# A graph network's first projection: seven half products for a pair of tiles, and counts shared between two engines

## The chip, the cores and the metric

The kernel runs on one core of one Trainium2 chip. The engines named here are TensorE (PE in the profile; PEld are its weight loads), VectorE (DVE), ScalarE (ACT), GpSimd (POOL) and SyncE (SP), which only issues DMAs. Each engine works through its own queue in order. The metric is device time in microseconds (us) of one execution; 10 runs of the kernel before the change had a median of 5349.94 us (5346.88 to 5354.68).

## The reference, cut to what matters

Two graph attention layers over 10,000 nodes with 170,000 edges (self loops among them, and one more a node in each layer), fp32, each with a residual product and layer norms. The change touches the first projection only, and the preparation of the edge lists that runs beside it:

```python
xl = (x @ W).reshape(n, heads, out_ch)          # x: 10000 x 768, W1: 768 x 1024
alpha_src = jnp.einsum('nhc,hc->nh', xl, a_src)  # 4 heads of 256
alpha_dst = jnp.einsum('nhc,hc->nh', xl, a_dst)
e = jax.nn.leaky_relu(alpha_src[src] + alpha_dst[dst], 0.2)
```

## The kernel before, in words

The nodes lie in NT = 79 tiles of 128 rows. The first stage (lines 602 to 670) makes `table1`: for each node the 1024 products with W1 plus b1, and 4 + 4 sums with a_dst and a_src. Then two stages gather rows of the tables by edge lists and do the rest; the change does not touch them.

The first stage is written out by hand: within `manual_schedule()` each engine's instructions stand in the order of the code. For each tile t:

- TensorE: `product` (L171) multiplies x's six transposed blocks of 128 x 128 with W1 (`w1`, held in SBUF) in two halves of 512 columns, 12 fp32 matmuls. PSUM has room for two such results (`ps_big`), so TensorE can be one tile ahead.
- ScalarE copies the result into `row` (L657). VectorE multiplies it in PSUM with a_dst and a_src spread over the partitions (L660, into `scr`, two buffers), and ScalarE sums each head's 256 numbers (L663, four per product, each with a readout of the accumulator).
- GpSimd adds b1 to `row` (L665). SyncE stores the row (L667). SyncE's load of x for tile t + 2 (`load_x`, L610, three buffers) stands ahead of that store.
- `next(steps)` (L668) then gives out one step of the preparation (`prepare`, L190) and one of the weights (`weight_steps`, L627). These steps stand in the same queues, between one tile's work and the next's. They come in this order: step 3 reads the edges' targets on VectorE and loads W2 on SyncE, step 4 makes a table of 1408 block ends by eleven transposes (L216, L217); steps 5 to 31 make 80 counts of how many block ends lie below a node's number, three in a step (L239, one pass over 1408 numbers on VectorE, summed by the instruction), turn them into addresses (`at`, L241), have GpSimd gather the blocks (L244) and look at the blocks of the step before (`remainder`, L230, L232). Steps 4 to 19 also multiply a block of W2 on VectorE (L642) and sum it on ScalarE (L643); step 19 loads Wr1, step 20 multiplies br1 with W2 on TensorE (L646). Steps 32 to 40 sort nodes by degree (L276, and L323 to L330 in groups with products on TensorE), steps 37 to 50 scatter the order with GpSimd's DMAs, six in a step (L313); steps 52 to 56 read it back on SyncE in pieces of 16 bytes (L344) and store ranks (L347); steps 57 to 76 gather the lists of sources, four DMAs of GpSimd in a step (L392), and VectorE works on them (`listed`, L365) a step later.

Of the kernel before, what the change touches and what calls it, by code (L numbers as in the profile page):

```python
# [79 lines left out]
def gnn_kernel(ctx, tc, x, x_cols, src, dst, src_col, dst_col, W1, a_src1, a_dst1, b1, g1, be1, Wr1, br1,  # L80
# [109 lines left out]
    def prepare():  # L190

        with tc.tile_pool(name="prep", bufs=1, side="right") as pool, \
                tc.tile_pool(name="prep2", bufs=2, side="right") as pool2:
            rows = pool.tile([P, NA, P], I32, name="rows")
            nc.sync.dma_start(rows, bass.AP(tensor=dst.tensor, offset=0, ap=[[P, P], [P * P, NA], [1, P]]))
            nxt = pool.tile([P, NA, P], I32, name="nxt")
            nc.sync.dma_start(nxt, bass.AP(tensor=dst.tensor, offset=1, ap=[[P, P], [P * P, NA], [1, P]]))
            info = pool.tile([P, NT, 4], I32, name="info")
            nc.vector.memset(info, 0)
# [1 line left out]
                nc.sync.dma_start(d.rearrange("(p j) f -> p (j f)", p=P), info.rearrange("p j f -> p (j f)"))  # L201
            yield
            yield
            fall = pool2.tile([P, NA * P], F32, name="less", bufs=1).rearrange("p (a e) -> p a e", e=P)
            nc.vector.tensor_tensor(fall, rows, nxt, op=OP.subtract)
            wrong = pool.tile([P, 3], F32, name="wrong")
            nc.vector.reduce_max(wrong[:, 0:1], fall.rearrange("p a e -> p (a e)"), axis=AX.X)
# [6 lines left out]
            for a in range(NA):  # L214
# [4 lines left out]
            ids = pool.tile([P, NB], F32, name="ids")  # L219
            nc.gpsimd.iota(ids, pattern=[[1, NB]], base=0, channel_multiplier=NT,  # L220
                           allow_small_or_imprecise_dtypes=True)
            whole = pool.tile([P, NB], F32, name="whole")
            rest = pool.tile([P, NB], F32, name="rest")
            at = pool.tile([P, NB], I32, name="at")
# [10 lines left out]
            for j in range(0, NB, STEP):  # L235
                m = min(STEP, NB - j)
                for i in range(j, j + m):
                    less = pool2.tile([P, NA * P], F32, name="less", bufs=1)
                    nc.vector.tensor_scalar(less, most.rearrange("p a e -> p (a e)"), ids[:, i:i + 1], 0.0,  # L239
                                            op0=OP.is_lt, op1=OP.add, accum_out=whole[:, i:i + 1])  # L240
                nc.vector.tensor_copy(at[:, j:j + m], whole[:, j:j + m])  # L241
                chunk = pool2.tile([P, STEP, P], I32, name="chunk")
                for i in range(m):
                    nc.gpsimd.indirect_dma_start(  # L244
                        out=chunk[:, i, :], out_offset=None, in_=dst.rearrange("(c e) o -> c (e o)", e=P),
                        in_offset=bass.IndirectOffsetOnAxis(ap=at[:, j + i:j + i + 1], axis=0))
                for r in asked:
                    remainder(*r)
                asked = [(j, m, chunk)]
                yield  # L250
            for r in asked:
# [18 lines left out]
            hot = pool.tile([P, NT, D], BF16, name="hot")  # L270
            nc.vector.tensor_tensor(hot, key[:, :, None].to_broadcast([P, NT, D]),
                                    node[:, None, :D].to_broadcast([P, NT, D]), op=OP.is_equal)
            before = pool.tile([P, NT + 1, D], BF16, name="before")
            nc.vector.memset(before[:, 0, :], 0.0)
            for j in range(NT):
                nc.vector.tensor_add(before[:, j + 1, :], before[:, j, :], hot[:, j, :])  # L276
# [9 lines left out]
            facts = pool.tile([P, NT, 4], I32, name="facts")  # L286
# [9 lines left out]
            base = each  # L296
            s = 1
            while s < D:
                more = pool.tile([P, D], F32, name=f"more{s}")
# [38 lines left out]
            yield  # L338

            sorted_ = pool.tile([P, NT, 4], I32, name="sorted_")  # L340
            others = [pool.tile([P, NT, 4], I32, name=n) for n in ("rows", "nxt", "info")]
# [258 lines left out]
    w2, wr1 = (wp.tile([P, k, n], F32, name=s) for s, k, n in (("w2", K1, R2), ("wr1", K0, C1)))  # L600

    with tc.tile_pool(name="w1", bufs=1) as w1p, tc.tile_pool(name="l1", bufs=2) as io, \
            psum_for_products(), tc.manual_schedule():
        w1 = w1p.tile([P, K0, C1], F32, name="w1")
        xTs = {}

        def load_x(t):
            if t < NT:
                xTs[t] = io.tile([P, K0, P], F32, name="xT", bufs=3)
                nc.sync.dma_start(xTs[t], x_cols[t])  # L610
# [16 lines left out]
        def weight_steps():  # L627

            with nc.allow_non_contiguous_dma(reason="1024 numbers"):
                nc.scalar.dma_start(br1_c, br1.rearrange("(k p) -> p k", p=P))
            yield
            yield
            brT = spread_br1(w1p, "brT")
            load(w2, W2)
            for i, a in enumerate((a_dst2, a_src2)):
                vec = spread(w1p, a, "a2")
                for k in range(K1):
                    yield  # L640
                    m = io.tile([P, C1], F32, name="scr")[:, :C2]
                    nc.vector.tensor_mul(m, w2[:, k, :C2], vec)  # L642
# [3 lines left out]
            q = product(brT, w2, R2)  # L646
            row = io.tile([P, R1], F32, name="row")
            nc.scalar.copy(row[:, :R2], q[:, :R2])
            nc.vector.tensor_add(lift, row[:, C2:C2 + 1], row[:, C2 + 1:R2])
            nc.scalar.dma_start(shift, row[0:1, :C2])  # L650


        steps = itertools.zip_longest(prepare(), weight_steps())
        for t in range(NT):
            p = product(xTs.pop(t), w1, C1)
            row = io.tile([P, R1], F32, name="row")
            nc.scalar.copy(row[:, :C1], p[:, :C1])  # L657
            for i, vec in enumerate((ad_b, as_b)):
                m = io.tile([P, C1], F32, name="scr")
                nc.vector.tensor_mul(m, p[:, :C1], vec)  # L660
# [4 lines left out]
            nc.gpsimd.tensor_add(row[:, :C1], row[:, :C1], b1_b)  # L665
            load_x(t + 2)
            nc.sync.dma_start(table1[t * P:(t + 1) * P, :R1 - 1], row[:, :R1 - 1])  # L667
            next(steps, None)  # L668
        for _ in steps:
            pass  # L670
# [613 lines left out]
```

## Time and profile before

| what | us |
| --- | --- |
| median of 10 runs | 5349.94 |
| the profiled execution, whole | 5356.32 |
| its span, first to last instruction | 5354.5 |
| last ScalarE sum of the first stage ends | 885.7 |
| TensorE busy with the tiles' products (L171, W1), 1896 records | 826.7 |
| VectorE's counts (L239), 80 of 1676 ns | 134.1 |
| GpSimd's bias adds (L665), 79 of 2369 ns | 187.2 |
| ScalarE's head sums (L663), 632 of 402 ns, and their readouts, 632 of 187 ns | 253.5 and 117.9 |

A tile's product with W1 has two records for each fp32 matmul, so 24. A row of the timeline reads: start, duration, engine and line, operation, output<-input, shapes, and in brackets how long the engine was idle just before and which event ended that. A name with a q (SPq) is an engine's queue issuing a DMA. The table by stretch gives for each stretch of the span the busy time of each engine, the granted clock of TensorE and what the DMA engines did. The view of DMA issues gives the size and the median time from issue to landing.

### The profile page before, as it was taken

What the parts mean: (1) busy time and instruction counts of PE and PEld (TensorE: products, weight loads), DVE (VectorE), ACT (ScalarE), POOL (GpSimd) and SP (SyncE); (2) the same over time, 40 slices, a digit from 0 to 9 for tenths busy, and PEclk for the clock granted to TensorE, in tenths of its full rate; (3) what the DMA queues carried; (4) which work ended last, traced back from release to release, by engine and by line L of the source; (5) the groups of instructions that cost most, each with busy time, mean ns of one, the idle gap of its engine ahead of it and who ended that gap; (6) DMA issues with size and microseconds to landing.
All of it is one profiled execution on the core that took longest, in us unless ns stands there. A gap on an engine that the chain in (4) does not pass through costs nothing. (4 is left out here: it accounts for less than half of the span.)

```text
span 5354.5 us, 59565 instructions
## 1 busy us (share of the span) xinstructions
PE 4762.7 (89%) x15188; PEld 2853.2 (53%) x15191; DVE 4283.1 (80%) x7729; ACT 2799.0 (52%) x8184; POOL 3227.1 (60%) x3159
## 2 busy tenths in 40 slices
PE   8999997999999886578999999999998865889998
PEld 3444443555555544345555555566665544566665
DVE  4884244899999888688899999689988767889998
ACT  3434343677778776577878777433333222323332
POOL 3446455455666654556666655277777656777774
PEclk9999998999999988789999999999999887999999
DMA  4333625899999997699999999599999989999995
GB/s 156 124 101 84 97 87 190 313 335 345 360 362 361 360 333 293 237 326 342 351 366 364 356 338 335 179 386 376 376 370 346 328 269 321 330 353 371 365 387 218
DMA packets 474306, 1591.37 MB, mean 297 GB/s; under 512 B 118327, under 2 KB 122487, under 8 KB 473958
## 3 DMA queue, kind: packets, MB, share of 16 engines
q0 software_dynamic: 322384, 1286.62, 66.3%
q1 hardware_dynamic: 149520, 297.43, 16.7%
q10 hardware_dynamic: 2054, 3.42, 0.2%
q8 instruction: 128, 2.10, 0.2%
q14 instruction: 220, 1.80, 0.1%
HBM read 1431.80 MB, written 177.29 MB: 301 GB/s over the span
## 5 line engine op out<-in xcount | busy, mean ns | idle before, releaser
L424 POOL DMA_INDIRECT ring<-table,slots x2675 | 2647.3, 990 | 1438.9 <-DVE acc L519 337.7
L519 DVE SCALAR_TENSOR_TENSOR acc<-ring,e,acc 128x512 f32<-128x512 f32 (+1 forms) x2530 | 1578.0, 624 | 126.2 <-PE acc L729 50.7
L508 ACT ACTIVATE ring<-ring,e 128x256 f32<-128x256 f32 x3284 | 1337.4, 508 | 0.0
L515 DVE TENSOR_TENSOR acc<-acc,ring 128x1024 f32<-128x1024 f32 x801 | 985.6, 1230 | 79.5 <-ACT ring L508 10.6
L928 PE MATMUL big<-ring,diagonals 128*128 128x256 f32 x2754 | 679.1, 409 | 203.4 <-ACT diagonals L927 194.3
L171 PE MATMUL big<-w,xT 128*128 128x512 f32 x1896 | 826.7, 598 | 27.2 <-DMA w<-in_W_dram 9.8
L171 PE MATMUL big<-wr,xT 128*128 128x512 f32 x1896 | 832.5, 596 | 0.2 <-ACT xT L700 0.2
L817 PE MATMUL half<-w,hT 128*128 128x512 f32 (+1 forms) x2528 | 830.4, 486 | 0.0
L942 PE MATMUL big<-wr,w 128*128 128x512 f32 (+1 forms) x2464 | 823.2, 487 | 0.0
L928 PEld LDWEIGHTS big<-ring,diagonals 128*128 128x128 f32 x2754 | 559.1, 206 | 320.5 <-ACT diagonals L927 222.2
L817 PEld LDWEIGHTS half<-w,hT 128*128 128x128 f32 x2528 | 477.8, 189 | 372.7 <-issue 310.0
L729 PE MATMUL acc<-ring,diagonals 128*128 128x256 f32 x1912 | 484.3, 412 | 212.0 <-ACT diagonals L723 212.0
L942 PEld LDWEIGHTS big<-wr,w 128*128 128x128 f32 x2464 | 469.7, 191 | 329.9 <-issue 298.0
L171 PEld LDWEIGHTS big<-w,xT 128*128 128x128 f32 x1896 | 362.3, 192 | 487.6 <-issue 468.3
L171 PEld LDWEIGHTS big<-wr,xT 128*128 128x128 f32 x1896 | 356.2, 191 | 419.9 <-issue 419.3
L729 PEld LDWEIGHTS acc<-ring,diagonals 128*128 128x128 f32 x1912 | 391.8, 208 | 296.9 <-ACT diagonals L723 234.5
L576 ACT ACTIVATE sd<-mv,eps 128x1 f32<-128x1 f32 x237 | 69.6, 294 | 821.6 <-DVE mv L574 821.5
L927 ACT ACTIVATE diagonals<-ident,e 128x128 f32<-128x128 f32 x1377 | 411.1, 387 | 142.1 <-DVE e L499 129.7
L660 DVE TENSOR_TENSOR scr<-big,ad_b 128x1024 f32<-128x1024 f32 x79 | 96.7, 1224 | 380.7 <-ACT row L657 380.7
L723 ACT ACTIVATE diagonals<-ident,e 128x128 f32<-128x128 f32 x956 | 292.8, 387 | 203.6 <-DVE e L499 203.2
L485 ACT ACTIVATE e<-e 128x68 f32<-128x68 f32 (+29 forms) x160 | 38.2, 239 | 659.8 <-DVE e L484 631.8
L665 POOL TENSOR_TENSOR row<-row,none 128x1024 f32<-128x1024 f32 x79 | 187.2, 2369 | 267.3 <-ACT row L657 266.9
(172 smaller groups left out, 3614.0 us busy)
## 6 DMA issues: line engine op xcount, KB each, us to landing
ring<-table,slots POOLq DMA_INDIRECT x2675, 6.9
table<-row SPq DMA_DIRECT2D x79, 516.0 KB, 3.7
h_d<-hT SPq DMA_DIRECT2D x79, 512.0 KB, 6.8
w<-h_d SPq DMA_DIRECT2D x77, 512.0 KB, 8.5
table<-row SPq DMA_DIRECT2D x79, 385.0 KB, 7.2
ring<-table SPq DMA_DIRECT2D x79, 385.0 KB, 6.6
xT<-in_x_cols_dram SPq DMA_DIRECT2D x79, 384.0 KB, 4.5
x_d<-xt SPq DMA_DIRECT2D x79, 384.0 KB, 7.6
```

The costliest lines, as they stand in the source:

```text
L171: nc.tensor.matmul(p[:, c:e], aT[:, j, :], w[:, j, c:e], start=(j == 0), stop=(j == k - 1))
L424: nc.gpsimd.indirect_dma_start(out=to, out_offset=None, in_=table, in_offset=bass.IndirectOffsetOnAxis(ap=index, axis=0), **more)
L508: nc.scalar.activation(row[:, s], row[:, s], AF.Copy, scale=e[:, h:h + 1])
L515: nc.vector.tensor_add(acc[:, :c], acc[:, :c], row[:, :c])
L519: nc.vector.scalar_tensor_tensor(acc[:, s], row[:, s], e[:, h:h + 1], (acc if first is None else first)[:, s], op0=OP.mult, op1=OP.add)
L665: nc.gpsimd.tensor_add(row[:, :C1], row[:, :C1], b1_b)
L723: nc.scalar.activation(diagonals[:, k * H1 + i, :], ident, AF.Copy, scale=e[:, k, i:i + 1])
L729: nc.tensor.matmul(acc[:, c:d], diagonals[:, k * H1 + i, :], ring.slot(q + k)[:, c:d], start=(k == 0 and c % BANK == 0), stop=(k == m - 1 ...
L817: nc.tensor.matmul(q, hT[:, j, :], w2[:, j, c:c + q.shape[1]], start=(j == 0), stop=(j == K1 - 1))
L927: nc.scalar.activation(diagonals[:, k % G, :], ident, AF.Copy, scale=e[:, k, :])
L928: nc.tensor.matmul(to, diagonals[:, k % G, :], ring.slot(FIRST[t] + k)[:, ON_PE2:C2], start=False, stop=(k == n - 1), skip_group_check=True)
L942: nc.tensor.matmul(r[:, c:d], hT[:, j, :], wr2[:, j, c:d], start=False, stop=(j == K1 - 1 and (d < C2 or not whole(t))), skip_group_check= ...
```

## The change

The rows of two tiles (t, t + 1), the two halves of the 768 inputs and the two halves of the 1024 columns make a 2 x 2 by 2 x 2 product of blocks. Strassen's scheme makes it from seven half products (3 matmuls of 512 columns each, 21 for two tiles in place of 24), each of a sum or difference of blocks of x with one of blocks of W1. Tile 0 is done alone, then 39 pairs.

- W1's five sums and differences are made once on VectorE, two of them in place after tile 0's product.
- x's five sums and differences (128 x 384 each) are made on VectorE for each pair, one pair ahead (`pair`).
- The seven results are combined on VectorE with seven additions or subtractions of 128 x 512 and on ScalarE with two copies. The seventh product is added by TensorE to m1's bank after m1 was read. Six PSUM banks (`ps_m`) take the place of the two double ones; `row` has four buffers.
- `finish` does what followed the product before, now from `row` in SBUF. The loads of x for the next pair stand behind the first two products of this pair.
- In each count step the counts with an even number are made on ScalarE: `Sign` with the sum of the instruction, then a short `Copy` that turns the sum of signs into a count. The output that nobody reads (`less`) is bf16 with two buffers.
- br1's product with W2 uses the new banks, and `brT` a buffer of `scr`. Some tiles of the preparation share buffers by taking each other's names.

```diff
             for j in range(0, NB, STEP):
                 m = min(STEP, NB - j)
                 for i in range(j, j + m):
-                    less = pool2.tile([P, NA * P], F32, name="less", bufs=1)
-                    nc.vector.tensor_scalar(less, most.rearrange("p a e -> p (a e)"), ids[:, i:i + 1], 0.0,
-                                            op0=OP.is_lt, op1=OP.add, accum_out=whole[:, i:i + 1])
+                    less = pool2.tile([P, NA * P], BF16, name="less")
+                    if i % 2:
+                        nc.vector.tensor_scalar(less, most.rearrange("p a e -> p (a e)"), ids[:, i:i + 1], 0.0,
+                                                op0=OP.is_lt, op1=OP.add, accum_out=whole[:, i:i + 1])
+                        continue
+                    nc.scalar.activation(less, most.rearrange("p a e -> p (a e)"), AF.Sign, scale=-1.0,
+                                         bias=halves[:, i:i + 1], accum_out=whole[:, i:i + 1])
+                    nc.scalar.activation(whole[:, i:i + 1], whole[:, i:i + 1], AF.Copy, bias=0.5 * NA * P, scale=0.5)
                 nc.vector.tensor_copy(at[:, j:j + m], whole[:, j:j + m])
...
-        for t in range(NT):
-            p = product(xTs.pop(t), w1, C1)
-            row = io.tile([P, R1], F32, name="row")
-            nc.scalar.copy(row[:, :C1], p[:, :C1])
...
+        def finish(t, row):
             for i, vec in enumerate((ad_b, as_b)):
                 m = io.tile([P, C1], F32, name="scr")
-                nc.vector.tensor_mul(m, p[:, :C1], vec)
+                nc.vector.tensor_mul(m, row[:, :C1], vec)
                 for h in range(H1):
                     s = slice(h * DH1, (h + 1) * DH1)
                     nc.scalar.activation(m[:, s], m[:, s], AF.Copy,
                                          accum_out=row[:, C1 + i * H1 + h:C1 + i * H1 + h + 1])
             nc.gpsimd.tensor_add(row[:, :C1], row[:, :C1], b1_b)
+            nc.sync.dma_start(table1[t * P:(t + 1) * P, :R1 - 1], row[:, :R1 - 1])
...
+        def times(a, b, p=None):
+            to = ps_m.tile([P, BANK], F32, name="m")[:, :NH] if p is None else p
+            for k in range(a.shape[1]):
+                nc.tensor.matmul(to, a[:, k, :], b[:, k, :], start=(p is None and k == 0),
+                                 stop=(k == a.shape[1] - 1), skip_group_check=True)
+            return to
...
+        bsums = w1p.tile([P, 3, KH, NH], F32, name="bsums")
+        for to, a, op, b in ((bsums[:, 0], b11, OP.add, b22), (bsums[:, 1], b11, OP.add, b12),
+                             (bsums[:, 2], b21, OP.add, b22), (b12, b12, OP.subtract, b22),
+                             (b21, b21, OP.subtract, b11)):
+            nc.vector.tensor_tensor(to, a, b, op=op)
+        finish(0, row)
+        next(steps, None)
+
+        def pair(t):
+            a1, a2 = (xTs.pop(i) for i in (t, t + 1))
+            a11, a12, a21, a22 = (a[:, k, :] for a in (a1, a2) for k in (upper, lower))
+            sums = io.tile([P, 5, KH, P], F32, name="sums")
+            for i, (a, op, b) in enumerate(((a11, OP.add, a12), (a21, OP.add, a22), (a11, OP.add, a22),
+                                            (a21, OP.subtract, a11), (a12, OP.subtract, a22))):
+                nc.vector.tensor_tensor(sums[:, i], a, b, op=op)
+            return a11, a22, sums
+
+        ready = pair(1)
+        for t in range(1, NT, 2):
+            a11, a22, sums = ready
+            r1, r2 = new_row(), new_row()
+            m3 = times(a11, b12)
             load_x(t + 2)
-            nc.sync.dma_start(table1[t * P:(t + 1) * P, :R1 - 1], row[:, :R1 - 1])
+            m5 = times(sums[:, 0], b22)
+            nc.scalar.copy(r1[:, right], m5)
+            load_x(t + 3)
+            m2 = times(sums[:, 1], b11)
+            nc.scalar.copy(r2[:, left], m2)
+            nc.vector.tensor_sub(r2[:, right], m3, r2[:, left])
+            m4 = times(a22, b21)
+            nc.vector.tensor_sub(r1[:, left], m4, r1[:, right])
+            nc.vector.tensor_add(r1[:, right], r1[:, right], m3)
+            nc.vector.tensor_add(r2[:, left], r2[:, left], m4)
+            if t + 2 < NT:
+                ready = pair(t + 2)
+            m1 = times(sums[:, 2], bsums[:, 0])
+            nc.vector.tensor_add(r2[:, right], r2[:, right], m1)
+            m6 = times(sums[:, 3], bsums[:, 1])
+            nc.vector.tensor_add(r2[:, right], r2[:, right], m6)
+            times(sums[:, 4], bsums[:, 2], m1)
+            nc.vector.tensor_add(r1[:, left], r1[:, left], m1)
+            finish(t, r1)
+            next(steps, None)
+            finish(t + 1, r2)
             next(steps, None)
```

More of the change, by code (lines that the diff above doesn't have):

```diff
@@ L193, in prepare @@
                 tc.tile_pool(name="prep2", bufs=2, side="right") as pool2:
-            rows = pool.tile([P, NA, P], I32, name="rows")
+            both = pool.tile([P, 2, NA, P], I32, name="hot")
+            rows, nxt = both[:, 0], both[:, 1]
             nc.sync.dma_start(rows, bass.AP(tensor=dst.tensor, offset=0, ap=[[P, P], [P * P, NA], [1, P]]))
-            nxt = pool.tile([P, NA, P], I32, name="nxt")
             nc.sync.dma_start(nxt, bass.AP(tensor=dst.tensor, offset=1, ap=[[P, P], [P * P, NA], [1, P]]))
@@ L203, in prepare @@
             yield
-            fall = pool2.tile([P, NA * P], F32, name="less", bufs=1).rearrange("p (a e) -> p a e", e=P)
+            fall = pool.tile([P, NA, P], F32, name="most")
             nc.vector.tensor_tensor(fall, rows, nxt, op=OP.subtract)
@@ L221, in prepare @@
                            allow_small_or_imprecise_dtypes=True)
+            halves = pool.tile([P, NB], F32, name="halves")
+            nc.vector.tensor_scalar_add(halves, ids, -0.5)
             whole = pool.tile([P, NB], F32, name="whole")
@@ L272, in prepare @@
                                     node[:, None, :D].to_broadcast([P, NT, D]), op=OP.is_equal)
-            before = pool.tile([P, NT + 1, D], BF16, name="before")
+            before = pool.tile([P, NT + 1, D], BF16, name="most")
             nc.vector.memset(before[:, 0, :], 0.0)
@@ L285, in prepare @@
             nc.vector.tensor_scalar(lower, node, number, None, op0=OP.is_gt)
-            facts = pool.tile([P, NT, 4], I32, name="facts")
+            facts = pool.tile([P, NT, 4], I32, name="info")
             nc.vector.memset(facts, 0)
@@ L298, in prepare @@
             while s < D:
-                more = pool.tile([P, D], F32, name=f"more{s}")
+                more = pool.tile([P, D], F32, name="more", bufs=2)
                 nc.vector.tensor_add(more[:, :D - s], base[:, :D - s], base[:, s:])
@@ L340, in prepare @@
             sorted_ = pool.tile([P, NT, 4], I32, name="sorted_")
-            others = [pool.tile([P, NT, 4], I32, name=n) for n in ("rows", "nxt", "info")]
+            others = [pool.tile([P, NT, 4], I32, name=n) for n in ("hot", "most", "info")]
             with nc.allow_non_contiguous_dma(reason="16 bytes a node"):
@@ L602, in gnn_kernel @@
     with tc.tile_pool(name="w1", bufs=1) as w1p, tc.tile_pool(name="l1", bufs=2) as io, \
-            psum_for_products(), tc.manual_schedule():
+            tc.tile_pool(name="ps_m", bufs=6, space=PSUM) as ps_m, \
+            tc.tile_pool(name="ps_tr", bufs=2, space=PSUM) as ps_tr, tc.manual_schedule():
         w1 = w1p.tile([P, K0, C1], F32, name="w1")
@@ L634, in weight_steps @@
             yield
-            brT = spread_br1(w1p, "brT")
             load(w2, W2)
@@ L645, in weight_steps @@
             yield
-            q = product(brT, w2, R2)
-            row = io.tile([P, R1], F32, name="row")
-            nc.scalar.copy(row[:, :R2], q[:, :R2])
+            brT = spread_br1(io, "scr")
+            row = io.tile([P, R1], F32, name="row", bufs=4)
+            for c in range(0, R2, BANK):
+                q = ps_m.tile([P, BANK], F32, name="m")[:, :min(BANK, R2 - c)]
+                for k in range(K1):
+                    nc.tensor.matmul(q, brT[:, k, :], w2[:, k, c:c + q.shape[1]],
+                                     start=(k == 0), stop=(k == K1 - 1))
+                nc.scalar.copy(row[:, c:c + q.shape[1]], q)
             nc.vector.tensor_add(lift, row[:, C2:C2 + 1], row[:, C2 + 1:R2])
@@ L653, in gnn_kernel @@
         steps = itertools.zip_longest(prepare(), weight_steps())
-        for t in range(NT):
-            p = product(xTs.pop(t), w1, C1)
-            row = io.tile([P, R1], F32, name="row")
-            nc.scalar.copy(row[:, :C1], p[:, :C1])
+        KH, NH = K0 // 2, C1 // 2
+        assert NT % 2 and K0 % 2 == 0 and NH <= BANK
+        upper, lower = slice(0, KH), slice(KH, K0)
+        left, right = slice(0, NH), slice(NH, C1)
+        b11, b12, b21, b22 = (w1[:, k, n] for k in (upper, lower) for n in (left, right))
+        def finish(t, row):
             for i, vec in enumerate((ad_b, as_b)):
                 m = io.tile([P, C1], F32, name="scr")
-                nc.vector.tensor_mul(m, p[:, :C1], vec)
+                nc.vector.tensor_mul(m, row[:, :C1], vec)
                 for h in range(H1):
@@ L665, in gnn_kernel, with new_row @@
             nc.gpsimd.tensor_add(row[:, :C1], row[:, :C1], b1_b)
-            load_x(t + 2)
-            nc.sync.dma_start(table1[t * P:(t + 1) * P, :R1 - 1], row[:, :R1 - 1])
+            nc.sync.dma_start(table1[t * P:(t + 1) * P, :R1 - 1], row[:, :R1 - 1])
+        def new_row():
+            return io.tile([P, R1], F32, name="row", bufs=4)
+        def times(a, b, p=None):
[4 more added lines that the diff above has]
+            return to
@@ new lines, in gnn_kernel @@
+        row = new_row()
+        x0 = xTs.pop(0)
+        for n in (left, right):
+            nc.scalar.copy(row[:, n], times(x0, w1[:, :, n]))
+        load_x(2)
+        bsums = w1p.tile([P, 3, KH, NH], F32, name="bsums")
[3 more added lines that the diff above has]
+            nc.vector.tensor_tensor(to, a, b, op=op)
```

## The prediction

> **What bounds the kernel now.** The change lies in the first stage: the last of the tiles' ScalarE sums ends at 885.7 us of the span of 5354.5. I read the table by stretch first, for the engine that is never idle there.
>
> ```profile
> core 0: us, PE busy (x) PEld busy (x) DVE busy (x) ACT busy (x) POOL busy (x), PEclk, DMA share, GB/s
> 150.00:200.00 50.00, 47.03 (x109) 20.06 (x108) 39.91 (x54) 22.37 (x79) 24.94 (x19) 1.00 0.33 108
> 550.00:600.00 50.00, 50.00 (x118) 22.07 (x117) 11.78 (x10) 21.57 (x85) 25.21 (x19) 1.00 0.33 86
> ```
>
> TensorE is busy throughout in the quiet stretch, at clock 1.00. Early, VectorE is at 80%: there the counts run. The timeline shows who ends a tile there (VectorE, one tile):
>
> ```profile
> 131.35 1.22 DVE L660 TENSOR_TENSOR scr<-big,ad_b 128x1024 f32<-128x1024 f32 x1 [1.90 <-ACT row L657]
> 132.49 1.21 DVE L660 TENSOR_TENSOR scr<-big,as_b 128x1024 f32<-128x1024 f32 x1
> 133.62 1.67 DVE L239 TENSOR_SCALAR_CACHE_REDUCE less<-most,ids 128x1408 f32<-128x1408 f32 x1
> ...
> 138.78 0.17 DVE L241 CAST at<-whole 128x3 int32<-128x3 f32 x1
> 138.89 0.56 DVE L230 TENSOR_TENSOR below<-chunk,ids 128x384 f32<-128x384 int32 x1
> 139.48 0.55 DVE L232 TENSOR_REDUCE rest<-below 128x3 f32<-128x384 f32 x1
> 139.95 0.95 DVE L642 TENSOR_TENSOR scr<-w,a 128x768 f32<-128x768 f32 x1
> 142.80 1.22 DVE L660 TENSOR_TENSOR scr<-big,ad_b 128x1024 f32<-128x1024 f32 x1 [1.90 <-ACT row L657]
> ```
>
> One tile takes 11.45 us (131.35 to 142.80) while counts and the sums over W2 both run. Elsewhere it is the 10.30 us of SyncE's stores, which also show SyncE's order: store, then the load for a later tile.
>
> ```profile
> 576.35 0.33 SPq L667 DMA_DIRECT2D table<-row  x1
> 576.77 0.38 SPq L610 DMA_DIRECT2D xT<-in_x_cols_dram  x1
> 586.65 0.33 SPq L667 DMA_DIRECT2D table<-row  x1
> 587.07 0.38 SPq L610 DMA_DIRECT2D xT<-in_x_cols_dram  x1
> ```
>
> **What TensorE saves.** 1896 records are 79 tiles x 12 products x 2 passes: 10.30/24 = 0.429 us a pass. A pair goes from 48 passes (20.6) to 42 (18.02): 2.58 x 39 = 101 us, if TensorE stays the bound.
>
> **Why it doesn't: a closed loop in each pair.** By the diff's order, the seventh product adds into m1's bank, so it waits for VectorE's add of m1. That add is queued behind the five sums of the next pair. They need x of the next two tiles, whose loads are issued in this same pass of the loop, on SyncE behind the store of the previous pair's second row. That store waits for GpSimd's bias add, which now waits for VectorE's two products (they read the row, no longer PSUM), which wait for the last add of the previous pair's seventh product. Before, the load was issued two tiles ahead and nothing on TensorE waited for VectorE except to reuse PSUM. So a pair lasts as long as the longer of TensorE (18.02), the VectorE chain V and the load chain X, with 0 = start of a pair's first 128x1024 product.
>
> Prices. A 128x1024 product: next starts 1.14 later; 128x512 from PSUM: 0.68 (row of L326), 0.60 with the overlap of 0.08; 128x384: 0.55, so 0.47. Four ScalarE sums: 121.16 to 122.77 = 1.61. Bias add 2.37. A count on ScalarE is not in the trace: from L663 and L643 (0.40 a piece at 256, 0.84 at 768: 0.86 ns an element) 1408 gives 1.39, and with the accumulator's 0.1 and the short Copy's 0.2 I take 1.7; bounds 1.2 and 2.1 from the 1.0 of a 1024 copy (L657) and twice L643. A count on VectorE 1.72, the rest of a count step 0.11 + 1.06. That `less` is now bf16 I cost at nothing: at half of L239's time VectorE would only wait longer for ScalarE's counts; the shared buffer names move no instruction. VectorE to TensorE 0.2 (L217 to L216).
>
> Common end: add of m1 0.65 + 0.2 + seventh product 2.58 + its add 0.60 = 4.0. V = (VectorE or ScalarE free after the second step) + four combinations 2.4 + five sums 2.35 + 4.0 = that + 8.8.
> X: the second store starts at B; store and load issue 0.42 each; landing of the second load; four sums 1.9; 4.0. The view of DMA issues:
>
> ```profile
> xT<-in_x_cols_dram SPq DMA_DIRECT2D x79, 384.0 KB, 4.5
> wr<-in_Wr_dram SPq DMA_DIRECT2D x2, 3072.0 KB, 10.2
> w<-in_W_dram SPq DMA_DIRECT2D x1, 3072.0 KB, 13.5
> ```
>
> Each 4.5 stands behind one store; the second of two loads also has the first ahead of it, 384 KB, so I take 5.2 (bounds: the 3.7 of the quickest xT, the 8.5 of ad_b). X = B + 0.84 + 5.2 + 5.9 = B + 12.0.
>
> **Pairs, by what preparation puts between the rows.**
> - Counts alone (pairs 11-14): products to 2.28; ScalarE's sums to 4.47. Step 1: two VectorE counts to 5.7, one ScalarE count to 6.15, rest to 7.3. Products to 9.6; ScalarE's sums to 11.8, its two counts to 15.2, where VectorE waits 3.9; rest to 16.4. V = **25.2** (20.6 before). The moved counts bring VectorE nothing: it waits for them, behind ScalarE's sums.
> - Counts and W2 sums (3-8): 0.87 twice on VectorE, 0.84 on ScalarE, behind which m5's and m2's copies (0.5 + 0.6) stand: those end at 20.2. V = **29.0** (22.9).
> - Scatters (19-24): GpSimd's order in the timeline is
>
> ```profile
> 445.65 2.36 POOL L665 TENSOR_TENSOR row<-row,none 128x1024 f32<-128x1024 f32 x1 [1.26 <-ACT row L657]
> 448.17 0.99 POOL L313 DMA_INDIRECT order_d<-facts,to  x1 [0.16 <-issue]
> ...
> 456.81 2.36 POOL L665 TENSOR_TENSOR row<-row,none 128x1024 f32<-128x1024 f32 x1 [1.29 <-ACT row L657]
> ```
>
>   First add 2.4 to 4.8, six scatters of 1.27 to 12.5, second add: B = 14.9, X = **26.9**.
> - Source lists (29-38): four gathers of 1.26 in place of the six: B = 12.35, X = **24.3**; V = 13.4 + 5.8 = 19.2 is shorter.
> - Quiet (25): `scr` has two buffers, so the third product waits for ScalarE to 3.0, the fourth to 4.6; second add 5.8 to 8.2; with one scatter B = 8.5, X = **20.5**, hardly under 20.6.
> - Single ones. Pair 1: W2's load (13.5) stands before x: 30. Pair 2: eleven transposes wait for VectorE, then a count: 27.5. Pair 9: Wr1's load (10.2): 31.6. Pair 10: the product with W2 (10.4) starts only after the first count step, at 8.0, then m3 to m7: 37.2. Pair 15: two counts in step 2: 23.5. Pair 16: 17.2 + 9.2 of small VectorE steps (375.54 to 392.74; 395.00 to 404.18), V = 4.6 + 26.4 + 8.8 = 39.8. Pair 17: 6.5 of them, B = 13.5: 25.5. Pair 18: 7.1, B = 14.5: 26.5. Pairs 26, 27: 16-byte loads before each store and load, which held SyncE 6 us each (597.86, 6.71): 30 each. Pair 28: the store of ranks, whose followers landed 21.2 later: 34.4.
>
> **The sum.** Pair 1's first product starts near 48: tile 0's product ends at 23.4, W1's sums are 5 x 1.67 (1536 elements at 1.04 ns), two of them behind that product, then 18 of TensorE and x of tiles 3, 4 behind preparation's loads. 48 + 30 + 27.5 + 6 x 29.0 + 31.6 + 37.2 + 4 x 25.2 + 23.5 + 39.8 + 25.5 + 26.5 + 6 x 26.9 + 20.5 + 2 x 30 + 34.4 + 10 x 24.3 = 1083.7. The last two rows: 2.3 + 4.3 of lists + 2.3, ScalarE and GpSimd to 11.2: 1094.9, so **209 us after** 885.7. Nothing behind the stage changes in the code. Profiled execution: 5356.3 (span 5354.5 and 1.8 around it) + 209 = 5565; on the median, 5349.9 + 209 = **5559**.
>
> [...] In the trace L660 runs at 24.51 and 25.65 beside GpSimd's add at 24.56 at its usual 1.22 and 1.21; it reads PSUM and SBUF. [...]
>
> **Rivals.**
> - *The loads keep ahead, V alone holds* (5410). If x lands before the sums are reached, pairs 1, 20-27 last 18.2, list pairs 19.2, pair 17 19.9, pairs 9 and 28 29.0; 18 and 19 keep 26 and 24 by TensorE behind VectorE's group steps. The stage ends near 946, 60 later. For it: V's terms are all measured. Against: SyncE's order above. 13%.
> - *TensorE stays the bound* (5238, faster): 48 + 38 x 18.06 + 28 (10.4 for the product with W2, 7 for the transposes, some 10 for the group products) + 11.2 = 774, 112 earlier. It wins as soon as a pair averages under (885.7 - 48 - 11.2)/38 = 21.75. Against: count, scatter and list pairs, 26 of the 38, come out at 24 and more. 6%; near the break-even 3%.
> - *Sign is dearer than a Copy* (5663). The trace has one ACT_TABLE_LOAD, 1.28, for a stage that uses Copy alone. If each count needed two switches at 1.28, 13.5 pairs x 3 counts x 2.56 = 104 us more. 8%. [...]
>
> **Numbers.** The forecast has 70%. Its own bounds: landings -27 to +59 (18 load-bound pairs x 1.5, x 3.3), counts -18 to +18 (13.5 pairs x 3 x 0.45), the four pairs whose loads are held -42 (as a quiet one) to +32 (14.7 for each 6.7 in pairs 26, 27): 5472 to 5668. The range 5405 to 5640 takes in the first rival, and leaves out the others and the far end: some 2 in 10. Faster by over 0.2% (what a measurement of this kernel can tell) 6%, within 3%, slower 91%.
>
> **What would show it.** VectorE's first sum of a quiet or scatter pair released by the DMA of xT; idle before the seventh product, with VectorE's add as releaser; the cast of `at` waiting some 4 us for ScalarE in every other count step; a TensorE share near 70% in place of 100%. If instead TensorE has no gaps in the quiet stretch, the loop is not closed and the prediction is wrong.

## The result, and the profile after

| | us |
| --- | --- |
| median of 8 runs after | 5673.36 (5663.18 to 5680.02) |
| median of 28 runs before | 5349.93 |
| ratio, with its 95% interval | 1.0603 [1.0594, 1.0613] |
| forecast (range) | 5559 (5405 to 5640) |
| span of the profiled execution, before and after | 5354.5, 5667.0 |
| first stage ends (the table load behind its last ScalarE sum), before and after | 885.7, 1205.2 |
| what follows, before and after | 4468.8, 4461.8 |

The direction was right and the size was short by 110 us: the stage became 319.5 longer where 209 were forecast, and what follows it became 7 shorter. The line numbers have shifted: the stage's products and head sums are L677 and L680, the bias add L682, the store L683, x's load L618, the half products L692, the additions of m1 and m6 to `row` L738 and L740, the seventh product's own addition L742.

The table by stretch, in the count stretch shown of before and in a stretch with scatters (busy time of PE, PEld, DVE, ACT and POOL, then the clock, DMA share, GB/s):

```profile
150.00:200.00 50.00, 31.65 (x67) 13.24 (x65) 31.38 (x47) 25.72 (x80) 22.68 (x16) 0.85 0.30 98
700.00:750.00 50.00, 40.47 (x84) 17.36 (x84) 24.20 (x27) 15.10 (x68) 27.64 (x22) 0.86 0.14 48
```

TensorE fell from 47 and 50 of 50 us to 32 and 40, and no other engine took its place: in the first row every engine is idle for over a third of the time, and in the second TensorE, still the busiest, for a fifth and all others for nearly half or more. That is the picture of a loop of waits and not of a busy engine. The clock column is the second thing to see: 1.00 before, 0.85 now. The waits by engine name the loop's joint:

```profile
PE m L692 <- DVE row L738: 329.4, 36, 21.4
```

In 36 waits TensorE stood 329.4 us for VectorE's addition of m1. One scatter pair on VectorE shows what that addition itself stands behind:

```profile
704.67 0.69 DVE L742 TENSOR_TENSOR row<-row,m 128x512 f32<-128x512 f32 x1 [3.68 <-PE m L692]
...
708.44 2.99 DVE L677 TENSOR_TENSOR scr<-row,ad_b 128x1024 f32<-128x1024 f32 x1 [0.69 <-ACT scr L680]
...
725.34 0.56 DVE L716 TENSOR_TENSOR sums<-xT 128x384 f32<-128x384 f32 x1 [6.99 <-DMA xT<-in_x_cols_dram]
726.69 1.99 DVE L716 TENSOR_TENSOR sums<-xT 128x384 f32<-128x384 f32 x4 [0.79 <-DMA xT<-in_x_cols_dram]
728.60 0.67 DVE L738 TENSOR_TENSOR row<-row,m 128x512 f32<-128x512 f32 x1
...
734.56 0.69 DVE L742 TENSOR_TENSOR row<-row,m 128x512 f32<-128x512 f32 x1 [4.49 <-PE m L692]
```

The addition of m1 (728.60) comes right behind the sums, the sums wait 7 us for x, and x's loads stand on SyncE behind the two stores, which wait for GpSimd; SyncE and GpSimd in the same pair:

```profile
710.38 11.03 SPq L683 DMA_DIRECT2D table<-row  x2
721.50 1.22 SPq L618 DMA_DIRECT2D xT<-in_x_cols_dram  x2
```

```profile
707.99 2.36 POOL L682 TENSOR_TENSOR row<-row,none 128x1024 f32<-128x1024 f32 x1 [8.48 <-DVE scr L677]
710.50 1.80 POOL L320 DMA_INDIRECT order_d<-info,to  x1
...
718.70 2.35 POOL L682 TENSOR_TENSOR row<-row,none 128x1024 f32<-128x1024 f32 x1
```

Both loads left 0.1 after the second store. Two durations in these rows are new: a product of 2.99 beside the bias add (the others of this pair take 1.22), and a scatter of 1.80 (most others 0.97). TensorE in the same pair:

```profile
714.77 5.31 PE L692 MATMUL m<-bsums,sums 128*128 128x512 f32 x12
729.33 5.19 PE L692 MATMUL m<-bsums,sums 128*128 128x512 f32 x6 [9.25 <-DVE row L738]
734.36 1.88 PE L692 MATMUL m<-w,xT 128*128 128x512 f32 x4
```

Twelve passes take 5.31 while TensorE is busy; after 9.25 us without work, six passes take 5.19, half the speed; the granted clock was 1.00 from 715 to 720 and 0.52 from 729.40 to 734.30. In a count pair the loop has the same end, and VectorE's chain instead of the loads ahead of it:

```profile
417.46 1.67 DVE L242 TENSOR_SCALAR_CACHE_REDUCE less<-most,ids 128x1408 bf16<-128x1408 f32 x1
...
423.15 0.17 DVE L248 CAST at<-whole 128x3 int32<-128x3 f32 x1 [4.01 <-ACT whole L247]
...
429.18 0.68 DVE L738 TENSOR_TENSOR row<-row,m 128x512 f32<-128x512 f32 x1
...
434.67 0.69 DVE L742 TENSOR_TENSOR row<-row,m 128x512 f32<-128x512 f32 x1 [4.01 <-PE m L692]
```

VectorE waits 4.01 for ScalarE's counts, as forecast (3.9), and 4.01 for the seventh product.

### The profile page after: what moved, and what is told of

Read it like the earlier page. It is cut to its first block, busy times and chain, and to the rows that moved or that the text cites. A ratio compares the mean times of both kernels' runs of the same rounds, so it can differ in the third digit from the quotient of the medians.

```text
span 5667.0 us, 59717 instructions
## 1 busy us (share of the span) xinstructions
PE 4740.5 (84%) x14954; PEld 2832.8 (50%) x14957; DVE 4554.5 (80%) x8123; ACT 2826.1 (50%) x8306; POOL 3270.9 (58%) x3159
## 5 line engine op out<-in xcount | busy, mean ns | idle before, releaser
L692 PE MATMUL m<-bsums,sums 128*128 128x512 f32 x702 | 384.2, 701 | 329.4 <-DVE row L738 329.4
L680 ACT ACTIVATE scr<-scr 128x256 f32<-128x256 f32 x632 | 253.5, 402 | 739.1 <-DVE scr L677 739.1
L682 POOL TENSOR_TENSOR row<-row,none 128x1024 f32<-128x1024 f32 x79 | 188.7, 2389 | 622.8 <-DVE scr L677 359.8
L692 PEld LDWEIGHTS m<-bsums,sums 128*128 128x128 f32 x702 | 153.9, 226 | 544.8 <-DVE row L738 361.3
```

What stands on the lines that cost most here:

```text
L692: nc.tensor.matmul(to, a[:, k, :], b[:, k, :], start=(p is None and k == 0), stop=(k == a.shape[1] - 1), skip_group_check=True)
```

## The experiments

A pair's period is the distance between two L742 (or the line that answers to it); the gap is from the end of the last addition of m1 to `row` to the start of L742, so it holds the handover and the seventh product. After the change the gap's mean is 4.64. Ratios are to the kernel before on the same chip. That took 5338 and 5342 us on the first two chips and 5632 and 5660 on the last two, where the later stages are some 300 longer. So stages are compared by their own ends, and totals by ratios; the changed kernel itself was not measured again on these chips.

**Single edits of the changed kernel.**

*x's loads a pair earlier* (the theory: x is late):

```diff
-                xTs[t] = io.tile([P, K0, P], F32, name="xT", bufs=3)
+                xTs[t] = io.tile([P, K0, P], F32, name="xT", bufs=4)
...
-            load_x(t + 2)
-            load_x(t + 3)
...
+            load_x(t + 4)
+            load_x(t + 5)
             if t + 2 < NT:
                 ready = pair(t + 2)
```

> Edit to the changed kernel: four buffers for x, and both loads of a coming pair issued one pair earlier, right behind m4, so ahead of the stores of the two rows; a few small buffers of the preparation shared to make room. Theory (the load chain closes the loop of quiet, scatter and held pairs): VectorE's first sum no longer waits for the DMA of xT; scatter pairs fall from 29.9 to 19-20 us (7 x 10), pairs 26-28 and 1 by some 38 together, list pairs by 1-3 each (VectorE is nearly as late there): some 130 us faster, 5540. Rival (VectorE's own queue and the clock set the pairs, the loads only happen to be late): within 20 us of 5673.

5566.95, ratio 1.0428 [1.0411, 1.0446]; the stage ends at 1103.8, 101 earlier, less than the 130 expected. No sum of a pair waits for x any more, scatter pairs from the third on last 23.9 in place of 29 to 30.5, quiet ones 19.6, count pairs 27.4 to 28.0 as before, where VectorE holds them. The gap stays (mean 4.37). So x's lateness is worth about 100 of the 320; the rest stays when x is early.

*Spare work for TensorE* (the theory: the seventh product runs slow because TensorE stood still). The result of these matmuls is not read:

```diff
+            idle = ps_tr.tile([P, BANK // P, P], F32, name="tr").rearrange("p a b -> p (a b)")
+            for _ in range(8):
+                nc.tensor.matmul(idle, sums[:, 3, 0, :], bsums[:, 1, 0, :], start=True, stop=True)
             times(sums[:, 4], bsums[:, 2], m1)
```

> Edit to the changed kernel: eight fp32 matmuls of 128x512 into a spare PSUM tile that nobody reads, between m6 and the seventh product, so that TensorE works (6.9 us) while it waits for VectorE. More work, no less waiting. Theory (TensorE falls to half clock in the wait of 7 to 9 us, and the seventh product is then paid at half clock): the time from the end of VectorE's add of m1 (L738) to its add of the seventh product (L742), 4.64 us in the mean, falls to 2.9, the granted clock of the stage rises from 0.84 to near 1.0, and the kernel is some 60 us faster, 5610. Rival (the seventh product is slow for another reason: weight loads behind the wait, PSUM or SBUF shared with VectorE): the same 4.6, no change or slower by up to 20.

5653.22, ratio 1.0591 [1.0574, 1.0609], a miss as a whole. Where the spare work filled the wait (pairs 11 to 14) the gap was 2.94 and the period 25.8 in place of 27.4 to 28.0. But pairs 2, 10, 18 and 19 rose to 33.9, 46.6, 38.1 and 34.8, each by 6 to 7. TensorE at the end of pair 10:

```profile
377.29 5.31 PE L692 MATMUL m<-bsums,sums 128*128 128x512 f32 x12
382.44 7.03 PE L743 MATMUL tr<-bsums,sums 128*128 128x512 f32 x16
389.31 2.74 PE L692 MATMUL m<-bsums,sums 128*128 128x512 f32 x6
```

There is no wait to fill here: in the changed kernel the seventh products at the end of these four pairs came at most 1 us after m6 (gap 2.93), because TensorE was itself the late engine, so the 7.0 us of spare work came on top. A queue for the spare work's buffers, which the next expectation names as the cause, doesn't show in the trace. That run has spare work only where the preparation doesn't want these buffers:

> Spare matmuls (128 x 512, result unread) stand between m6 and the seventh product only in the pairs where nothing of the preparation wants the two buffers that they write: twelve in pairs 3 to 9, eight in pairs 11 to 15, 20 to 25 and from 29 on, 29 pairs in all. Theory (TensorE, after 7 to 9 us without work, runs the seventh product's six passes at about half its clock): the gap from the end of VectorE's add of m1 to the seventh product's own add falls from 4.64 to about 2.9 in these pairs and stays in the others; 29 x 1.8 = 52 us less than the changed kernel, some 5620 us. In the first attempt the gain was eaten by pairs 2, 10, 18 and 19, which waited for the buffers; they should be back at 28, 40, 32 and 28. Rival (the gap is a cost of handing over between engines, whatever the clock): gap 4.6 everywhere, no change, some 5673.

5644.5, ratio 1.0564 [1.0546, 1.0581]; the stage ends at 1182.8, 22 earlier. TensorE in a count pair:

```profile
425.70 7.03 PE L746 MATMUL tr<-bsums,sums 128*128 128x512 f32 x16
433.35 2.84 PE L692 MATMUL m<-bsums,sums 128*128 128x512 f32 x6 [0.62 <-DVE row L738]
```

Behind the spare work the six passes take 2.84, where they took 4.71 in the changed kernel's count pair; the granted clock over such a pair is 1.00 in place of 0.88. In 24 of the 29 pairs with spare work the gap is 2.93 to 2.94, count pairs last 25.8 and list pairs 26.0 to 26.4 (27.4 to 28.0 and 27.8 to 29.5 in the changed kernel). The expected 52 came to 22, because pairs 2, 10, 19 and 38 became 29 us longer (to 37.0, 47.0, 35.1 and 24.9): the seventh product that ends each of them belongs to the next two tiles, which had spare work again, and there TensorE again had hardly a wait to fill (at most 1.1 us in the changed kernel). That the wait ahead of them makes these passes slow is shown: only spare work for TensorE was added, and where it filled the wait the same six passes went from 4.71 to 2.84.

*All counts on VectorE* (`if i % 2:` becomes `if True:`):

> Edit to the changed kernel: all 80 counts on VectorE again, the projection as changed. Theory (VectorE waits for ScalarE's counts about as long as it would take to make them): some 0.9 us a pair dearer over 13 pairs, 12 us slower, 5685; the cast of at no longer waits for ScalarE. Rival (what is taken off VectorE comes off the time): 40 counts of 1.72, up to 69 us slower, 5740.

5666.22, ratio 1.0612 [1.0595, 1.063], no difference from the whole change; stage 1205.6. The counts' half on ScalarE is worth nothing in this order.

*Without GpSimd's bias add* (the line of L682 left out, so the table lacks b1):

> Edit to the changed kernel: GpSimd's bias add is left out (b1 is added to no row). Theory (the add and VectorE's operations with two SBUF inputs shut each other out): L677's 2.98 in scatter pairs falls to 1.22 and L380's mean of 1.32 in list pairs to 0.24; with the add also gone from the load chain, scatter pairs fall from 29.9 to 20-22, list pairs by 2 to 3: some 90 us faster, 5580. Rival (only the load chain counts): the same fall of scatter pairs, list pairs as they are, some 60 us faster, and L677 and L380 slow as before.

5559.24, ratio 1.0413 [1.0392, 1.0433]; the stage ends at 1097.0, 108 earlier. Scatter pairs from the third on 19.8 to 22.7, list pairs 21.3 to 25.8, count pairs again 27.5 to 28.4. L677 and L380 are back at 1.22 and 0.23 in the mean, as the theory had it, and list pairs did fall, so the rival is out. The add costs by its time ahead of the store and by what it does to VectorE; how much each of the two costs this run can't tell.

**The loop opened by order alone.** TensorE makes m1 before m4, and VectorE takes it up first, so that the seventh product no longer stands behind the sums and x:

```diff
-            nc.vector.tensor_sub(r2[:, right], m3, r2[:, left])
+            m1 = times(sums[:, 2], bsums[:, 0])
+            nc.vector.tensor_sub(r2[:, right], m1, r2[:, left])
+            nc.vector.tensor_add(r2[:, right], r2[:, right], m3)
...
-            m1 = times(sums[:, 2], bsums[:, 0])
-            nc.vector.tensor_add(r2[:, right], r2[:, right], m1)
```

> Only an order changes: TensorE makes m1 before m4, and VectorE takes m1 up first, so the seventh product, which adds into m1's bank, no longer stands behind VectorE's five sums of the next pair and so behind that pair's x. Theory (the closed loop goes through m1's add): the seventh product follows m6 without a gap and at full clock; a pair is then the longer of VectorE's chain (end of the second step + 6.6 in place of + 8.8, and the 1.9 of the slow seventh product gone) and of the loads (second store + 9.3 in place of + 12.0): about 4 us less in each of 38 pairs, 150 less than the changed kernel, some 5520 us. Rival (TensorE and the seventh product are not on the path; VectorE and the loads alone set it): the pair still waits for x and VectorE, within 40 of the changed kernel, 5630 to 5673.

5501.01, ratio 1.0297 [1.028, 1.0314]; the stage ends at 1038.9, 166 earlier than after the change, with as many instructions of the same sizes. No L742 waits more than 0.2 for the seventh product. The same with x a pair earlier:

> As the kernel with m1 first, and the loads of x issued a pair earlier (four buffers for x; small buffers of the preparation shared). Theory: the load chain and the seventh product are both out of the loop, and VectorE with ScalarE alone hold a pair: scatter and quiet pairs at 18 to 20, list pairs 22 to 25, count pairs 23 to 25; a further 60 to 100 less than with m1 first alone, 5420 to 5460 us, still slower than before. Rival (one of the two was hidden behind the other): the gain of both together is hardly more than the larger of the two, 5520 to 5560.

5430.14, ratio 1.0165 [1.0148, 1.0182]; stage 969.8, 235 earlier than after the change; the two edits alone gave 101 and 166, so they overlap by 32. Scatter pairs (20 to 24) last 15.7 to 20.9, quiet ones 17.2 to 18.3 (but pair 25, 24.2), count pairs 23.5, list pairs 23.4 to 24.0. Now list pairs show what is left; VectorE and then GpSimd in one:

```profile
800.45 0.23 DVE L379 TENSOR_TENSOR eq<-window,key 128x76 f32<-128x76 int32 x1
800.72 2.35 DVE L380 TENSOR_TENSOR eq<-eq,below 128x76 f32<-128x76 f32 x1
803.11 0.28 DVE L381 TENSOR_TENSOR eq<-eq,far 128x76 f32<-128x76 f32 x1
...
805.36 1.22 DVE L677 TENSOR_TENSOR scr<-row,ad_b 128x1024 f32<-128x1024 f32 x1
806.49 1.22 DVE L677 TENSOR_TENSOR scr<-row,as_b 128x1024 f32<-128x1024 f32 x1
807.63 0.23 DVE L377 TENSOR_TENSOR below<-node,real 128x76 f32<-128x76 f32 x1
811.39 1.02 DVE L379 TENSOR_TENSOR eq<-window,key 128x76 f32<-128x76 int32 x1 [3.53 <-DMA window<-in_src_dram,begin]
```

```profile
800.62 2.36 POOL L682 TENSOR_TENSOR row<-row,none 128x1024 f32<-128x1024 f32 x1 [7.33 <-DVE below L377]
...
805.63 3.05 POOL L399 DMA_INDIRECT window<-in_src_dram,begin  x1 [0.30 <-issue]
```

An operation on 128 x 76 numbers takes 2.35 and ends as GpSimd's add does (802.98). The other way round, a gather's issue takes 3.05 in place of 0.94 beside VectorE's two products, and ends 0.97 after the second of them. And the second windows, for which VectorE waits 3.53, are gathered behind the add and behind that slow issue. To see what the add costs where no store holds up x any more, the bias add was left out of this kernel (the table lacks b1):

> The kernel with m1 first and x a pair early, without GpSimd's bias add (so the table lacks b1). In that kernel nothing waits for the add's latency any more, so what goes now is only what the add takes from VectorE while both read SBUF. Theory (they shut each other out for a whole instruction): in list pairs the step's operation on eq and below falls from 2.35 to 0.23 and VectorE's wait for the second window (3.5) shrinks by the 2.4 that the add stood ahead of the gathers: list pairs from 23.7 to 18.5 to 20, count pairs unchanged at 23.5 within 0.5; 35 to 60 us less, some 5370 to 5395 where the kernel before takes 5342. Rival (the add costs VectorE nothing, only its latency mattered): list pairs at 22 or more, less than 20 us in all.

5714.64, ratio 1.0099 [1.0084, 1.0115]. Eight of the nine list pairs last 17.7 to 18.0 in place of 23.4 to 24.0, TensorE's own 18.0 and less than expected; count pairs 23.5 as expected. The group of L380, first with the add and then without:

```profile
L380 DVE TENSOR_TENSOR eq<-eq,below 128x80 f32<-128x80 f32 (+13 forms) x20 | 26.3, 1315 | 0.7
```

```profile
L380 DVE TENSOR_TENSOR eq<-eq,below 128x80 f32<-128x80 f32 (+13 forms) x20 | 4.7, 234 | 0.7
```

These eight pairs became 46 us shorter. That is not L380 alone, whose 2.35 in place of 0.23 is some 2 us of the 5.8 in a pair: VectorE's waits for the windows also fell, from 31.2 us in 9 waits to 5.7 in one. The stage ended only 14 earlier, because pairs 18, 19 and 29 took 35.1, 69.4 and 28.6 in place of 31.1, 27.8 and 23.6. In pair 19, without the adds, GpSimd issued 64 scatters in one row, SyncE's two stores took 22.1 and two loads 27.8, the DMA engines moved 37 GB/s in place of 69, and ScalarE and VectorE stood still for up to 32.0 and 41.1. What released them the trace doesn't name, and that the scatters held up the large transfers is not shown: no run changed them alone.

**Versions meant to beat both.** The first: m1 first, x early, one step of the preparation in the middle of the pair and one at its end, the second row's products ahead of the seventh product's addition, one count of three on VectorE, addresses cast a step later:

```diff
+            load_x(t + 4)
+            load_x(t + 5)
+            if t + 2 < NT:
+                ready = pair(t + 2)
+            next(steps, None)
             nc.vector.tensor_sub(r1[:, left], m4, r1[:, right])
...
             nc.vector.tensor_add(r2[:, right], r2[:, right], m6)
+            finish(t + 1, r2)
             times(sums[:, 4], bsums[:, 2], m1)
             nc.vector.tensor_add(r1[:, left], r1[:, left], m1)
             finish(t, r1)
             next(steps, None)
```

> A version meant to beat both: m1 first, x a pair earlier, one step of the preparation in the middle of the pair (behind the next pair's sums) and one at its end, the second row's products ahead of the seventh product's add, one count of three on VectorE in place of every other, and addresses cast a step after their counts, so that VectorE does not wait for ScalarE. Theory (the loop and not the amount of work is what lost the time): count pairs 19 to 22, W2 pairs 21 to 23, scatter and quiet pairs 18 to 20, list pairs 20 to 23; the stage ends 40 to 100 earlier than the other kernel with x early, 5300 to 5400 us, near the kernel before or under it. [...]

5384.0, ratio 1.0073 [1.0056, 1.009]; stage 926.0. List pairs (21.4 to 22.5) and scatter pairs came as the theory had them, count pairs (22.8) and the pairs with counts and W2 sums (24.4) a little above, and the whole is still slower than before. VectorE in a count pair:

```profile
285.91 2.97 DVE L681 TENSOR_TENSOR scr<-row,ad_b 128x1024 f32<-128x1024 f32 x1
...
296.64 0.69 DVE L735 TENSOR_TENSOR row<-m,row 128x512 f32<-128x512 f32 x1 [3.10 <-DMA xT<-in_x_cols_dram]
```

The product of 2.97 stands beside the bias add. The 3.10 is put down to x's load, but L735 reads no x: ScalarE's copy into `row` ended at 296.55, behind two counts of the step before. Both are order again, so the next version puts ScalarE's copies ahead of the counts and brings each row's second product a pair later, ahead of the combinations that read PSUM:

```diff
             nc.scalar.copy(r2[:, left], m2)
+            if t > 1:
+                next(steps, None)
...
             if t + 2 < NT:
                 ready = pair(t + 2)
+            for args in left_over:
+                finish(*args)
             nc.vector.tensor_sub(r1[:, left], m4, r1[:, right])
...
+            headsums(r2, 0)
+            headsums(r1, 0)
+            left_over = [(t + 1, r2), (t, r1)]
```

> From the trace of the spread version (stage end 926.0): in a count pair VectorE waits 3.1 us for ScalarE's two copies, which stand behind the counts of the step before; the third product takes 2.97 beside GpSimd's bias add, and in a list pair the step's third operation 2.26 in place of 0.23; in pair 9 VectorE waits 14 for the product with W2. Here ScalarE's copies stand ahead of the step's counts, the second product of each row comes a pair later, just ahead of the combinations that read PSUM, so that both bias adds run beside those and beside a count, and the small sum after the product with W2 goes to GpSimd. Theory (order alone costs these): the product back at 1.22, count pairs from 22.8 to 18.5 to 20, list pairs from 21.6 to 18.5 to 20, W2 pairs from 24.4 to 20 to 22, pair 9 from 38.6 to 28 to 32, the stage ends near 860 and the whole is some 5280 to 5320, under the kernel before. Rival (VectorE's amount of work and not its waits sets the pairs): within 20 of the spread version, 5360 to 5390.

5616.19, ratio 0.9972 [0.996, 0.9984]; stage 856.7, 69 earlier than the version before it and 29 earlier than the kernel before. Count pairs last 18.1 to 18.5, most pairs with W2 sums 18.9, pair 9's work (now in pair 10) 34.3. List pairs (19.6 to 22.4) and scatter pairs (most at 21.2 to 21.7) missed; so did the whole (5280 to 5320 were expected where the kernel before takes 5342, a ratio of 0.988 to 0.996). It was run again to see whether the gain holds:

> The same kernel as the spread version with the bias adds covered, on whatever chip these runs get, to learn whether its gain over the kernel before holds where that takes 5342 and not 5632: the stage ended at 856.7 instead of 885.7 there, 29 us; if the rest is unchanged, 0.5% faster (ratio 0.993 to 0.998); if the later stages lose something by it, 0.998 to 1.001.

5637.85, ratio 0.9967 [0.9955, 0.9979]; stage 860.3, which differs by 3.6 from the same kernel on the chip before. The gain holds, but again where the kernel before takes over 5600, so what it is on the first two chips stays open. The last one moves the adds of list pairs behind the first gathers:

> The same with two orders changed: in list pairs the bias adds and stores stand behind the first gathers of the pair (VectorE waited 2 to 4 us for the windows behind them), and the first row of a pair is finished before the second (its buffer is the first that ScalarE wants again; in the scatter pairs VectorE waited 10 us for that copy). Theory: list pairs from 21.2 to 18.5 to 20, scatter pairs from 21.5 to 19 to 21: 15 to 30 us less than that version, ratio to before 0.988 to 0.994. Rival (GpSimd's queue holds these pairs whatever the order): within 8 us of that version.

5618.97, ratio 0.9931 [0.9916, 0.9945]: faster than the kernel before by 0.7%, again on a chip where that takes 5660, and 18.9 us less than the version before it on the same chip. The stage ends at 842.7, 43 earlier than before. List pairs went from 19.6 to 22.5 down to 19.2 to 19.6. Pairs 22 to 25 stayed at 21.4 to 21.7, so for those the rival holds: GpSimd's queue is full there (from 453.50 to 475.92 two adds and twelve scatters, no pause over 0.31). The count stretch now:

```profile
150.00:200.00 50.00, 49.26 (x115) 21.32 (x114) 49.62 (x77) 42.87 (x131) 30.99 (x23) 1.00 0.39 124
```

TensorE 49.3 and VectorE 49.6 of 50 at clock 1.00: here the scheme has what it promised, and both engines are full.

## Why the prediction was right, and where it was wrong

*The loop was right, point by point.* The four signs named in the prediction are there: sums released by x's DMA (98.0 us of waits), TensorE idle before the seventh product with VectorE's addition as releaser (329.4), the cast waiting 4.0 for ScalarE in every other step and 0.6 in the rest (62.3 in 27 waits), and TensorE's share in a count stretch at 63%. Opening the loop by order alone took back 166. The prices of the counts held too (on ScalarE one starts 1.69 after the other, against 1.7; no further table load), so the third rival fell; that its 5663 lies near the 5673 measured is chance. The first two rivals came true only where an edit made them so: VectorE alone in the kernel with m1 first and x early, TensorE in the list pairs without the bias add.

*What failed is the sum's common end, and in it the seventh product at 2.58.* Forecast: "add of m1 0.65 + 0.2 + seventh product 2.58 + its add 0.60 = 4.0". Measured: 0.68 + the gap's mean of 4.64 + 0.72 = 6.04. Three pairs by the prediction's own terms, each measured from its first product:

| | scatter pair, 705.39 to 735.28 | list pair, 1002.08 to 1031.59 | count pair, 407.74 to 435.39 |
| --- | --- | --- | --- |
| second store, or end of second step | 15.7 (14.9) | 14.3 (12.35) | 16.6 (16.4) |
| loads, or combinations and sums | 5.6 (6.04) | 6.4 (6.04) | 4.9 (4.75) |
| four sums | 1.9 (1.9) | 1.9 (1.9) | |
| common end | 6.7 (4.0) | 7.0 (4.0) | 6.2 (4.0) |
| period (forecast) | 29.9 (26.9) | 29.5 (24.3) | 27.7 (25.2) |

In each column the largest error is in the end. 2.04 us x 38 pairs = 77 of the missing 110. Of it 1.71 x 38 = 65 is the slow seventh product (a gap of 4.64 against the 2.93 of pairs whose wait was filled, which the second run with spare work shows); the rest is 0.15 a pair in the handover and the product at full speed (2.93 against 2.78) and as much in the two additions. The seventh product was priced at the full-speed row of the kernel before, though the same prediction had TensorE stand still just ahead of it. The trace of before had the sign, in its one long wait of the quiet stretch (TensorE idle 7.58 before 660.58): the stretch from 655 to 692 shows a granted clock of 0.86 between stretches of 1.00. In the runs here slow passes followed nearly every wait of over 3.5 us (226 of 227), and waits of 2.0 to 3.5 us about every other time (by size below).

*The second error was a price left out.* The forecast has VectorE's products start 1.14 apart beside GpSimd's add as well. In the row of before that it had for this, at 24.51, the product takes 1.22 beside the add, but has one input in PSUM; after the change both lie in SBUF. The trace of before has rows of that kind too. Two of the 79 additions of L276, which read two inputs in SBUF and take 0.19, stand beside GpSimd's add and last until it ends (2.23 and 2.27); GpSimd and VectorE in the first:

```profile
383.62 2.37 POOL L665 TENSOR_TENSOR row<-row,none 128x1024 f32<-128x1024 f32 x1 [7.94 <-ACT row L657]
383.80 2.23 DVE L276 TENSOR_TENSOR before<-before,hot 128x64 bf16<-128x64 bf16 x1
```

The trace after shows the same (a product of 2.99 in place of 1.22, L380 at 2.35 in place of 0.23). In list pairs the step's VectorE work meets the first add, and a gather's issue of 3.04 delays the second. That is the 1.9 in the first row of the list column; the nine list pairs were 38 over the forecast in all, 20 beyond their common end. The remaining 13 of the 110 are the start (4.5 late), the last two rows (1.7) and single pairs: pair 18 was 5.4 over in all and pair 9 4.5, pair 38 without lists 4.9 under.

*The range.* Its bounds had landings, counts and held loads, each from a row; the common end, in all 38 pairs, had no bound at all, and it was the term that failed.

## What to carry to other kernels

When a change makes TensorE wait, price what it does after the wait at the speed that a trace shows after such a wait: here 33 of 39 pairs ended in six passes of 4.2 to 5.5 us in place of 2.84. Filling such a wait with spare work pays only where there is a wait: in four pairs without one it cost its own time, 6 to 7 us each. Fewer instructions on the engine that is the bound bring nothing while a buffer that it must have back stands behind other engines' queues, so look first at the order in which that buffer is read and freed. The same instructions in another order went from a ratio of 1.060 to 1.030, and with loads, copies and adds placed by what they stand beside, and the counts divided anew, to 0.993 on another chip.

## What the runs showed of the hardware

- TensorE's speed after idle time, from 417 groups of six passes that began after a wait, in the first stages of the changed kernel and the twelve others: after less than 2.0 us all 129 took 2.84; after 2.0 to 3.5 us 29 of 61 took 2.81 to 2.84 and 32 took 4.15 to 5.49; after more than 3.5 us 226 of 227 took 4.16 to 5.49 and one, after 3.83, took 2.84.
- GpSimd's add and VectorE's operations with two inputs in SBUF took longer where they met, in both directions, down to operations of 0.23 us. In the changed kernel nine products that met an add took 2.82 to 2.99 in place of 1.22, and ten operations of L380 2.35 to 2.38 in place of 0.23. In the version with the adds covered, 32 adds that began during a product took 3.11 to 3.29 in place of 2.36, and each ended 2.2 after that product. A cast of the changed kernel (L337) took 2.62 in place of 0.17 and ended with the add. VectorE's combinations with one input in PSUM (0.68) and its count (1.67) ran beside it at their own times.
- A gather's issue on GpSimd was longer beside VectorE's products in SBUF as well: ten of the 79 for the lists in the changed kernel took 2.13 to 3.09 in place of 0.94, and each ended 0.8 to 1.0 after the second product. Before, where the products read PSUM, none of these 79 took over 1.01. It was the same without the bias add (3.19 to 3.45).
